# Turning a block's keys with VectorE and memory in a gated attention block: unscaled keys, scales applied on the way out of PSUM

## The chip, the cores and the metric

The kernel runs on one core of one Trainium2 chip. The metric is the device time of one execution in microseconds (us). Before the change the median of three runs was 1321.52 us (1321.27 to 1323.14).

## The reference, cut to what matters

All data are float32. There are 32 batches of 256 query tokens and 77 context tokens, 256 wide. A batch first passes a cross attention with 8 heads of 128 features, without softmax, and then a feed-forward part with 16 small heads and a softmax. The change touches the cross attention alone:

```python
f_q, f_k, f_v = proj(q), proj(k), proj(v)       # layer norm, @ w_in.T, 8 heads of 128; k and v are the same context
cosine_sim = dots / (qn[..., :, None] * kn[..., None, :])
q_ratio = 2.0 * minimum(q_var, 1.0) / (q_var + 1.0)      # k_ratio likewise
var_component = einsum('hqn,hqm->hqnm', q_ratio, k_ratio)
mixed = cw * cosine_sim + vw * cosine_sim * decorr_scale + ww * var_component
out = einsum('hqnm,hqmd->hqnd', mixed, f_v)               # then @ w_out.T + b_out
```

The weights `cw`, `vw`, `ww` and `decorr_scale` are one number for each head. So a score of head h, query n and key m is (dot of the query, divided by its norm, with the key) x (a scale of h and m) + (q_ratio of h and n) x (k_ratio of h and m, times `ww`). As keys and values are equal, the scale can be put on the keys, half (a square root) in the scores and half in the values, or wholly on the scores.

## The kernel before, in words

A preamble (to about 70 us of the profile) loads and turns the weights, normalizes the context and gathers the means that the head weights need. The batches then run in a software pipeline. The list `cycle`, written out by hand, gives the order of the stages of one round: an entry `(2, scale_keys)` in round n calls `scale_keys` for batch n + 2. `run` calls each stage once for each batch, so stages that the preamble has called are passed over. The last two rounds have lists of their own (`last_but_one`, `last`). Instructions of TensorE (`pe`), ScalarE (`act`), VectorE (`dve`) and GpSimd (`pool`) stay on their engine in the order of the program; the DMAs on SyncE's queue (`nc.sync`) are placed by the tile framework, and the profile shows some of them ahead of their place in the list.

Matmul results go to PSUM tiles: three tiles `mm` of 128 x 512, two tiles `sc` for the softmax scores, one `zp`. A float32 matmul is two MATMUL instructions in the trace, a transpose on TensorE is one.

For the context of batch b the stages are these. `key_features` multiplies a part of the normalized context by `w_in` (ScalarE copies it to `fvx`). `count_keys` and `measure_keys` take each token's variance and norm for each head. `align_keys` copies the 77 rows of the batch to `fv`, and their norms and ratios (16 numbers a row) to `nr`. `weigh_keys` multiplies these by the head weights `aw`. `scale_keys` (VectorE) lays the scales out as diagonal blocks `dk`. `transpose_keys` multiplies `fv` by `dk` on TensorE, eight matmuls of 96 columns (16 instructions), which turns and scales the keys in one step and adds the ratios as a column; ScalarE and VectorE copy one half each to `fvT`. `key_outputs` multiplies `fvT` by `w_out` into `vw`, in three stages: two in which each matmul fills 64 PSUM partitions with the first 64 (`MA`) keys of a head, and one (pair 2) with 32 partitions for the last 13 (`MR`) keys of all heads.

For the queries, `query_features` makes `fq`, `scale_queries` takes ratios and norms and divides by the norms (GpSimd), and `turn_queries` turns `fq`: from batch 2 on VectorE transposes blocks of 32 x 32, one DMA writes them to memory (`fd`) and `fetch_queries` reads them back in another order to `fqT`. The ratios ride along as a ninth head. `query_scores` has the same three stages as `key_outputs`; ScalarE and VectorE copy the results to `s`. `attend` multiplies `s` by `vw`, adds the residual, and the feed-forward part follows: `ff_stats`, `ff_norm`, `ff_transpose`, `ff_project`, `ff_values`, then four turns of `scores` (TensorE, then VectorE's maximum `nm`), `exponents` (ScalarE), `scale_values` (VectorE) and `mix_values` (TensorE), then `ff_out`, `ff_gelu` and `ff_add`.

Of the kernel before, what the change touches and what calls it, by code (L numbers as in the profile page):

```python
# [35 lines left out]
def gated_block_kernel(  # L36
# [59 lines left out]
    nquart = const.tile([P, H], F32, name="nquart")  # L96
    dve.memset(nquart, -0.25)
# [207 lines left out]
    def measure_keys(b):  # L305

        run(b, count_keys)
        for i in range(halves_due(b - 1) // 2, halves_due(b) // 2):
            rows = min(P, NCTX - i * P)
            nr = nrx[0:rows, i % 4, :]  # L310
            m2, n2, rt = head_stats(key_stats.pop(i), "k")
            pool.tensor_tensor(nr[:, 0:H], n2, nquart[0:rows], ALU.pow)
            dve.scalar_tensor_tensor(nr[:, H : 2 * H], m2, P - 1.0, rt, ALU.min, ALU.mult)

    def align_keys(b):
        k = kept[b]
        k["fv"] = sw.tile([P, 4, D], F32, tag="ct", name="fv", bufs=2).rearrange(
            "p a d -> p (a d)"
        )[0:M]
        k["nr"] = pa.tile([M, 2 * H], F32, tag="nr", name="nr")  # L320
        at = 0
        while at < M:
            i, row = divmod(b * M + at, P)
            n = min(P - row, M - at)
            nc.sync.dma_start(out=k["fv"][at : at + n], in_=fvx[i % 4][row : row + n])
            nc.sync.dma_start(out=k["nr"][at : at + n], in_=nrx[row : row + n, i % 4, :])
            at += n

# [6 lines left out]
    SL = MA + 32  # L335

    def weigh_keys(b):

        k = kept[b]
        k["dk"] = pa.tile([M, H // 2, 2, SL], F32, tag="dk", name="dk", bufs=1)  # L340
        pool.tensor_tensor(k["nr"], k["nr"], aw[0:M].rearrange("p w h -> p (w h)"), ALU.mult)

    def scale_keys(b):

        k = kept[b]
        dve.tensor_tensor(
            k["dk"],
            eyes.unsqueeze(1).to_broadcast([M, H // 2, 2, SL]),
            k["nr"][:, 0:H].rearrange("m (g i) -> m g i", i=2).unsqueeze(3).to_broadcast(
                [M, H // 2, 2, SL]  # L350
            ),
            ALU.mult,
        )
        for i in range(2):
            dve.tensor_copy(
                k["dk"][:, :, i, M + 16 * i], k["nr"][:, H + i : 2 * H : 2]
            )

    def transpose_keys(b, hh):
        k = kept[b]  # L360
        if hh == 0:
            k["fvT"] = pa.tile([P, H, SL], F32, tag="fvT", name="fvT", bufs=2)
        pt = mm_tile()
        for i in range(4):
            h = hh * 4 + i
            pe.matmul(
                pt[:, i * SL : (i + 1) * SL], lhsT=k["fv"][:, h * P : (h + 1) * P],
                rhs=k["dk"][:, h // 2, h % 2, :], start=True, stop=True,
            )
        out = k["fvT"][:, hh * 4 : hh * 4 + 4, :].rearrange("p h m -> p (h m)")  # L370
        (act.copy if hh == 0 else dve.tensor_copy)(out, pt[:, 0 : 4 * SL])

    def paired(pt, k, pair, rhs):

        for c in range(2):
            for i in range(2):
                h = 4 * pair + 2 * c + i
                pe.matmul(
                    pt[MA * i : MA * (i + 1), c * S : (c + 1) * S],
                    lhsT=k["fvT"][:, h, 0:MA], rhs=rhs(h), start=True, stop=True,  # L380
                )

    def key_outputs(b, pair):

# [5 lines left out]
        if pair < 2:  # L390
            paired(pg, k, pair, lambda h: woutT[:, h, :])
            out = k["vw"][:, 2 * pair : 2 * pair + 2, :].rearrange("p g c -> p (g c)")
            (act.copy if pair == 0 else dve.tensor_copy)(out, pg)
            return
        for i in (1, 0):
            for j in range(4):
                n = 32 if i else MR + 1
                pe.matmul(
                    pg[32 * j : 32 * j + n, 0:D], lhsT=k["fvT"][:, 2 * j + i, MA : MA + n],
# [4 lines left out]
    def query_scores(b, pair):  # L404

# [4 lines left out]
        if pair < 2:  # L410
            paired(pg, k, pair, lambda h: k["fqT"][:, :, h, :])
            out = k["s"][:, 2 * pair : 2 * pair + 2, :].rearrange("p g q -> p (g q)")
            (act.copy if pair == 0 else dve.tensor_copy)(out, pg)
            return
        for i in (1, 0):
            for j in range(4):
                n = 32 if i else MR
                pe.matmul(
                    pg[32 * j : 32 * j + n, 0:S], lhsT=k["fvT"][:, 2 * j + i, MA : MA + n],
                    rhs=k["fqT"][:, :, 2 * j + i, :], start=(i == 1), stop=(i == 0),  # L420
                )

        dve.scalar_tensor_tensor(
            k["s"][:, 4, :].rearrange("p (i a) -> p i a", a=32),
            pg[:, 0:S].rearrange("p (i a) -> p i a", a=32), scored[:, 0:1],
            k["fqT"][:, :, H, :], ALU.mult, ALU.add,
        )
# [21 lines left out]
    def scale_queries(b, t):  # L449
# [12 lines left out]
            qrps[t][:, :, MR], m2, P - 1.0, rt, ALU.min, ALU.mult  # L462
        )

    def turn_queries(b, t):
# [3 lines left out]
        if t == 0:  # L469
            k["fqT"] = pa.tile([P, S // 32, H + 1, 32], F32, tag="fqT", name="fqT", bufs=1)  # L470
        ratios = qrps[t].rearrange("p h w -> p (h w)")
        if b < 2:
# [11 lines left out]
            pt = mm_tile()  # L484
            pe.transpose(pt[:, 0:P], ratios, ident)
            dve.tensor_copy(
# [1091 lines left out]
```

## Time and profile before

| what | value |
|---|---|
| median of three runs | 1321.52 us |
| the profiled execution: its time, its span | 1320.74 us, 1318.7 us |
| busy PE / DVE / ACT / POOL | 1294.0 / 1042.7 / 880.6 / 508.7 us |
| granted TensorE clock | 0.999 |
| one round, from `mix_values` (u 3) to the next | 36.73 us in most rounds; 38.45 us with two halves of `key_features` |
| DMA queue q1 | 144.42 MB, 35.8% of 16 engines |

The profile names an instruction by engine, operation and tiles, `out<-in`, with its shape; `zp<-e,vz 128*32 128x256` is a matmul with 32 columns of weights and 256 moving columns. All instructions that go through the ordering helper carry its line, 32, so groups are told apart by tile. SPq is SyncE's queue of DMAs and shows the line of the DMA itself. The timeline merges neighbours of a kind: start, duration of the merged piece, and the count behind the x.

### The profile page before, as it was taken

To read this page: it belongs to the slowest core of one execution; us is meant where nothing else is said; L and a number is where in the kernel's file an instruction comes from. 1 tells how busy PE (TensorE), PEld (TensorE's weight loads), DVE (VectorE), ACT (ScalarE), POOL (GpSimd) and SP (SyncE) were. 2 spreads that over 40 slices of the span, in tenths; PEclk is the share of its full clock that TensorE was granted. 3 is DMA by queue.
4 is the path that set the end of the run, shared out by engine and by line. 5 is a ranking of instruction groups with operands and counts; after the bars stand their busy time and mean duration, and the time that the engine had idled before them with its cause. 6 is when DMAs were issued, how large, how long until landed. Compare 5 with 4: busy or idle time off the path is not lost.

```text
span 1318.7 us, 26220 instructions
## 1 busy us (share of the span) xinstructions
PE 1294.0 (98%) x8671; PEld 777.1 (59%) x8671; DVE 1042.7 (79%) x3071; ACT 880.6 (67%) x2856; POOL 508.7 (39%) x629
## 2 busy tenths in 40 slices
PE   8999999999999999999999999999999999999998
PEld 7865556665555556665555556665555555655554
DVE  7746788788788787888887887878887877888865
ACT  6822557677666767667666767676666767667666
POOL 6823443434334342435333443433433433343300
PEclk9999999999999999999999999999999999999999
DMA  8610034432244343433343443432343433432231
GB/s 279 212 35 22 20 113 122 127 115 98 83 129 127 118 126 115 125 116 100 95 120 120 129 123 119 126 115 94 95 127 120 126 116 102 133 98 85 69 97 41
DMA packets 99638, 146.11 MB, mean 111 GB/s; under 512 B 14170, under 2 KB 65039, under 8 KB 99502
## 3 DMA queue, kind: packets, MB, share of 16 engines
q1 hardware_dynamic: 98670, 144.42, 35.8%
q8 instruction: 69, 1.13, 0.4%
q14 instruction: 67, 0.55, 0.1%
q10 hardware_dynamic: 832, 0.00, 0.0%
HBM read 65.98 MB, written 68.16 MB: 102 GB/s over the span
## 4 chain that ended last, share of the span: by engine, by line
PE 91%; DVE 4%; DMA 3%; POOL 1%; ACT 1%; issue 1%; SPq 0%; ACTq 0%; DVEq 0%; POOLq 0%
PE mm L32 70%; PE sc L32 11%; PE zp L32 9%; DVE nm L32 1%; DMA x<-in_x_dram 1%; DVE st L32 1%; DMA w_in_n<-in_L_xattn_w_in_dram 1%; DVE qst L32 0%; DMA ct<-in_ctx_dram 0%; ACT e L32 0%; DVE qt L32 0%; DMA out_dram<-x 0%; POOL rstd_x L32 0%; DMA gcol<-in_L_xattn_ln_g_dram 0%; POOL rc L32 0%
## 5 line engine op out<-in xcount | busy, mean ns | idle before, releaser
L32 ACT ACTIVATE e<-sc,nm 128x256 f32<-128x256 f32 x1016 | 468.3, 483 | 221.2 <-DVE nm L32 221.1
L32 DVE TENSOR_REDUCE nm<-sc 128x4 f32<-128x1024 f32 x254 | 299.2, 1219 | 48.2 <-PE sc L32 48.1
L32 PE MATMUL mm<-winT,xTc 128*128 128x512 f32 x512 | 234.6, 599 | 0.3 <-ACT fqT L32 0.3
L32 ACT ACTIVATION_READ_ACCUMULATOR e<-sc,nm 128x1 f32 x1016 | 217.6, 214 | 0.0
L32 POOL TENSOR_TENSOR rq<-qt,nhalf 128x8 f32<-128x8 f32 x64 | 105.4, 1647 | 256.8 <-DVE qt L32 256.8
L32 PEld LDWEIGHTS mm<-winT,xTc 128*128 128x128 f32 x512 | 94.2, 190 | 105.3 <-issue 95.7
L32 PE MATMUL sc<-q,kTf 32*128 32x512 f32 x1016 | 147.6, 640 | 0.5 <-ACT kTf L32 0.5
L32 PE MATMUL mm<-vw,s 128*128 128x256 f32 x640 | 146.7, 384 | 0.0
L32 PE MATMUL zp<-e,vz 128*32 128x256 f32 x2048 | 137.0, 385 | 0.3
L32 PEld LDWEIGHTS mm<-vw,s 128*128 128x128 f32 x640 | 119.0, 190 | 28.4 <-issue 13.5
L32 POOL TENSOR_TENSOR fq<-fq,rq 128x1024 f32<-128x1024 f32 x64 | 121.4, 1897 | 5.0
L32 PEld LDWEIGHTS zp<-e,vz 128*32 128x32 f32 x2048 | 53.4, 109 | 105.0 <-issue 34.5
L32 POOL TENSOR_TENSOR nrx<-kt,nquart 128x8 f32<-128x8 f32 (+1 forms) x20 | 32.9, 1644 | 194.8 <-DVE kt L32 194.8
L32 DVE BATCH_NORM_STATS2 qst<-fq 128x6 f32<-128x128 f32 x512 | 104.7, 280 | 0.0
L32 PE MATMUL mm<-fqT,fvT 128*64 128x256 f32 (+2 forms) x1024 | 94.3, 385 | 3.5 <-DMA nr<-nrx 1.9
L32 PE MATMUL mm<-woutT,fvT 128*64 128x256 f32 (+2 forms) x1024 | 93.7, 382 | 1.5 <-ACT v L32 1.5
L32 DVE RECIPROCAL sums<-sums 128x8 f32<-128x8 f32 x128 | 23.7, 185 | 75.1 <-ACT e L32 75.1
L32 PEld LDWEIGHTS mm<-fqT,fvT 128*64 128x64 f32 (+2 forms) x1024 | 46.7, 119 | 58.6 <-DVE qst L32 22.0
L32 ACT ACT_TABLE_LOAD x60 | 77.0, 1283 | 4.9 <-DMA x<-in_x_dram 4.2
L32 POOL TENSOR_SCALAR xn<-x,mv_x,rstd_x 128x256 f32<-128x256 f32 x64 | 78.5, 1233 | 4.2 <-issue 4.2
L32 ACT COPY fvx<-mm 128x512 f32<-128x512 f32 (+1 forms) x40 | 23.5, 587 | 80.4 <-PE mm L32 80.4
L32 PE MATMUL mm<-winT,kT_all 128*128 128x512 f32 (+1 forms) x160 | 74.8, 598 | 0.0
(239 smaller groups left out, 2135.4 us busy)
## 6 DMA issues: line engine op xcount, KB each, us to landing
fd<-fb SPq DMA_DIRECT2D x60, 576.0 KB
fqT<-fd SPq DMA_DIRECT2D x240, 144.0 KB
x<-in_x_dram SPq DMA_DIRECT2D x64, 256.0 KB
x_kept<-x SPq DMA_DIRECT2D x32, 256.0 KB
z_kept<-zT SPq DMA_DIRECT2D x32, 256.0 KB
out_dram<-x SPq DMA_DIRECT2D x31, 256.0 KB
xd<-xb SPq DMA_DIRECT2D x29, 256.0 KB
xq<-xd SPq DMA_DIRECT2D x116, 64.0 KB
```

Of the source, the lines that this page charges most:

```text
L32: return lambda *args, **kw: self._tc.keep_in_program_order(method(*args, **kw))
```

## The change

Keys are no longer scaled before they are turned. `measure_keys` takes the full power -1/2 instead of -1/4. `align_keys` splits the last 13 keys over two sets of rows (even and odd heads), `turn_keys` turns the rows as `turn_queries` does (VectorE, memory, `fetch_keys`; TensorE in the first two batches). The scales and ratios travel through memory (`align_norms`, `fetch_norms`) into one number for each row of the score tiles, and the queries' ratios are spread through memory over those rows (`spread_ratios`, `sort_ratios`, `fetch_ratios`); GpSimd multiplies them (`weigh_ratios`). All five score tiles leave PSUM by a VectorE instruction that multiplies by the scale and adds that product. All products with `fvT` have 32 columns. Before the rounds, a square root on GpSimd (`hw`) is gone and four small VectorE instructions make `aw_rows`. In `cycle`, `turn_keys` stands near the start, `ff_gelu` and its table load before `scores` 2, and `scores` 3 before `ff_transpose`.

```diff
 def measure_keys(b):
-            pool.tensor_tensor(nr[:, 0:H], n2, nquart[0:rows], ALU.pow)
+            pool.tensor_tensor(nr[:, 0 : 2 * H : 2], n2, nhalf[0:rows, 0:H], ALU.pow)
...
+            if at < MA:
+                n = min(n, MA - at)
+                nc.sync.dma_start(out=k["fv"][at : at + n], in_=fvx[i % 4][row : row + n])
+            else:
+                for odd in range(2):
+                    to = at + 16 * odd
+                    nc.sync.dma_start(
+                        out=k["fv"][to : to + n].rearrange("m (g i d) -> m g i d", i=2, d=P)[
+                            :, :, odd
+                        ],
...
+    def align_norms(b):
...
+            nc.sync.dma_start(out=nr[at : at + n], in_=nrx[row : row + n, i % 4, :])
...
+        k["nd"] = nd = dram.tile([P, 5, 2], F32, tag="nd", name="nd")
+        for i in range(2):
+            nc.sync.dma_start(
+                out=nd[MA * i : MA * (i + 1), 0:4, :],
+                in_=nr[0:MA].rearrange("m (g i w) -> i m g w", i=2, w=2)[i],
+            )
+        nc.sync.dma_start(
+            out=nd[:, 4, :].rearrange("(h m) w -> m h w", m=16),
+            in_=nr[MA : MA + 16].rearrange("m (h w) -> m h w", w=2),
+        )
+    def fetch_norms(b):
...
+        nc.sync.dma_start(out=k["rows"], in_=k.pop("nd"))
 def weigh_keys(b):
+        k["wr"] = pa.tile([P, 5, 2], F32, tag="wr", name="wr")
+        pool.tensor_tensor(k["wr"], k["rows"], aw_rows, ALU.mult)
-    def scale_keys(b):
...
-    def transpose_keys(b, hh):
...
-                pt[:, i * SL : (i + 1) * SL], lhsT=k["fv"][:, h * P : (h + 1) * P],
-                rhs=k["dk"][:, h // 2, h % 2, :], start=True, stop=True,
...
+    def turn_keys(b):
+        k["fvT"] = pa.tile([P, 3, H, 32], F32, tag="fvT", name="fvT", bufs=2)
+        if b < 2:
...
+                    pe.transpose(
+                        pt[:, i * SL : (i + 1) * SL], k["fv"][:, h * P : (h + 1) * P],
+                        ident[0:SL, 0:SL],
+                    )
...
+        kb = pa.tile([P, 4, H, 32], F32, tag="fb", name="kb", bufs=2)[0:SL]
+        dve.transpose(
+            kb.rearrange("p j h a -> p h j a"),
+            k["fv"].rearrange("p (h j a) -> p h j a", j=4, a=32),
+        )
+        kd = dram.tile([SL, 4, H * 32], F32, tag="kd", name="kd")
+        nc.sync.dma_start(out=kd, in_=kb.rearrange("p j h a -> p j (h a)"))
+    def fetch_keys(b):
...
+        for j in range(4):
+            nc.sync.dma_start(
+                out=k["fvT"][32 * j : 32 * j + 32].rearrange("p i h a -> p i (h a)"),
+                in_=kd[:, j].rearrange("(i p) n -> p i n", p=32),
+            )
 def paired(pt, k, pair, rhs):
         for c in range(2):
-            for i in range(2):
-                h = 4 * pair + 2 * c + i
+            for j in range(4):
+                h = 4 * pair + 2 * c + j // 2
                 pe.matmul(
-                    pt[MA * i : MA * (i + 1), c * S : (c + 1) * S],
-                    lhsT=k["fvT"][:, h, 0:MA], rhs=rhs(h), start=True, stop=True,
+                    pt[32 * j : 32 * j + 32, c * S : (c + 1) * S],
+                    lhsT=k["fvT"][:, j % 2, h, :], rhs=rhs(h), start=True, stop=True,
 def key_outputs(b, pair):
-            (act.copy if pair == 0 else dve.tensor_copy)(out, pg)
+            act.copy(k["vw"][:, 2 * pair : 2 * pair + 2, :].rearrange("p g c -> p (g c)"), pg)
 def query_scores(b, pair):
-            (act.copy if pair == 0 else dve.tensor_copy)(out, pg)
...
+        for g in (2 * pair, 2 * pair + 1) if pair < 2 else (4,):
+            c = g % 2
+            dve.scalar_tensor_tensor(
+                k["s"][:, g, :], pg[:, c * S : (c + 1) * S], k["wr"][:, g, 0:1],
+                k["rq"][:, g, :], ALU.mult, ALU.add,
+            )
+    def spread_ratios(b):
+        rb = pa.tile([P, 32], F32, tag="rb", name="rb")
+        dve.transpose(rb, qrs[b % 2])
+        k["rc"] = dram.tile([P, 32], F32, tag="rc", name="rc")
+        nc.sync.dma_start(out=k["rc"], in_=rb)
+    def sort_ratios(b):
+        k["rd"] = dram.tile([H * NT, 4, 32], F32, tag="rd", name="rd")
+        nc.sync.dma_start(
+            out=k["rd"], in_=k.pop("rc").rearrange("(i c) a -> c i a", c=32)[0 : H * NT]
+        )
+    def fetch_ratios(b, first):
+        if first:
...
+            k["re"] = dram.tile([P, S], F32, tag="re", name="re")
...
+            k["rq"] = pa.tile([P, 5, S], F32, tag="rqr", name="rqr", bufs=1)
+            for i in range(2):
...
+                nc.sync.dma_start(
+                    out=k["rq"][MA * i : MA * (i + 1), 0:4, :],
+                    in_=src.unsqueeze(0).to_broadcast([MA, 4, S]),
+                )
+        else:
+            nc.sync.dma_start(out=k["rq"][:, 4, :], in_=k.pop("re"))
+    def weigh_ratios(b):
+        for g in range(5):
+            r = k["rq"][:, g, :]
+            if g < 4:
+                pool.tensor_scalar(r, r, k["wr"][:, g, 1:2], None, ALU.mult)
+            else:
+                pool.tensor_scalar(
+                    r, r, k["wr"][:, g, 1:2], ident[:, MR + 1 : MR + 2], ALU.mult, ALU.add
+                )
 def turn_queries(b, t):
-        dve.transpose(fb[:, :, H, :], ratios.rearrange("p (j a) -> p j a", a=32))
-        fd = dram.tile([P, 4, (H + 1) * 32], F32, tag="fd", name="fd")
+        fd = dram.tile([P, 4, H * 32], F32, tag="fd", name="fd")
...
-    run(0, scale_keys)
     run(0, scale_queries, 1)
-    run(0, transpose_keys, 0)
-    run(0, transpose_keys, 1)
+    run(0, spread_ratios)
+    run(0, sort_ratios)
+    run(0, fetch_ratios, True)
+    run(0, fetch_ratios, False)
+    run(0, weigh_ratios)
+    run(0, turn_keys)
...
     cycle = [
         (4, load_queries),
+        (1, fetch_ratios, False),
         (-1, mix_values, 3),
         (0, scores, 0),
         (2, measure_keys),
-        (2, align_keys),
         (3, norm_inputs),
         (0, exponents, 0, 0),
+        (2, align_keys),
         (-1, ff_out),
         (-1, ff_keep),
+        (2, turn_keys),
         (0, exponents, 0, 1),
...
+        (2, align_norms),
         (-1, ff_norm_inv),
+        (1, weigh_ratios),
         (0, scores, 1),
...
+        (2, fetch_keys),
...
         (3, transpose_inputs),
+        (2, fetch_norms),
+        (-1, ff_gelu),
+        (2, warm_exponentials),
+        (0, square_weights),
         (0, scale_values, 1),
-        (2, weigh_keys),
         (1, query_scores, 0),
...
-        (2, scale_keys),
         (1, attend, 0),
...
-        (2, transpose_keys, 0),
-        (2, transpose_keys, 1),
         (1, ff_norm, 1),
         (2, scale_queries, 1),
+        (2, spread_ratios),
         (3, key_features),
+        (0, scores, 3),
         (1, ff_transpose),
-        (-1, ff_gelu),
-        (2, warm_exponentials),
-        (0, scores, 3),
         (0, mix_values, 2),
-        (2, key_outputs, 2),
         (2, key_outputs, 0),
         (2, key_outputs, 1),
+        (2, key_outputs, 2),
         (2, turn_queries, 0),
+        (2, sort_ratios),
...
         (1, ff_project, "q"),
+        (2, weigh_keys),
...
         (2, fetch_queries, 0),
+        (2, fetch_ratios, True),
         (2, fetch_queries, 1),
...
```

## The prediction, made before the result was known

> **What bounds the kernel now.** I read the page first: the busy shares and the chain that ended last.
>
> ```profile
> PE 1294.0 (98%) x8671; PEld 777.1 (59%) x8671; DVE 1042.7 (79%) x3071; ACT 880.6 (67%) x2856; POOL 508.7 (39%) x629
> PE 91%; DVE 4%; DMA 3%; POOL 1%; ACT 1%; issue 1%; SPq 0%; ACTq 0%; DVEq 0%; POOLq 0%
> ```
>
> TensorE is busy for 98% of the span and carries 91% of the chain. Then the timeline of one round, which begins at the `zp` group (`mix_values`, u 3) at 551.23 and ends at the next one at 587.96:
>
> ```profile
> 551.23 1.07 PE L32 MATMUL zp<-e,vz 128*32 128x256 f32 x16
> 552.23 1.14 PE L32 MATMUL sc<-q,kTf 32*128 32x512 f32 x8
> ...
> 564.36 2.95 PE L32 MATMUL mm<-fqT,fvT 128*64 128x256 f32 x32
> 567.24 1.14 PE L32 MATMUL sc<-q,kTf 32*128 32x512 f32 x8
> 568.31 1.07 PE L32 MATMUL zp<-e,vz 128*32 128x256 f32 x16
> 569.31 4.58 PE L32 MATMUL mm<-vw,s 128*128 128x256 f32 x20
> 573.73 1.92 PE L32 MATMUL mm<-dk,fv 77*128 77x96 f32 x16
> 575.49 1.91 PE L32 MATMUL mm<-winT,kT_all 128*128 128x512 f32 x4
> 577.24 0.60 PE L32 MATMUL mm<-ident,xf 128*128 128x128 f32 x4
> 577.77 1.14 PE L32 MATMUL sc<-q,kTf 32*128 32x512 f32 x8
> 578.84 1.07 PE L32 MATMUL zp<-e,vz 128*32 128x256 f32 x16
> 579.73 2.92 PE L32 MATMUL mm<-woutT,fvT 128*32 128x256 f32 x32
> ```
>
> No piece waits: each starts where the one before ends. So a round is the sum of TensorE's work, 36.73 us, and what the change takes from TensorE comes off, until another engine is late. How near the others are, the table by stretches shows (us; PE, PEld, DVE, ACT and POOL busy, with counts):
>
> ```profile
> 551.23:587.96 36.73, 36.73 (x254) 21.55 (x253) 31.54 (x97) 25.75 (x86) 14.99 (x16) 1.00 0.39 118
> ```
>
> VectorE has 5.2 us to spare in such a round (in rounds that have no keys to count it works less: 28.8 in 245.38 to 282.11).
>
> **TensorE, step by step.** (1) The keys' product with `dk` goes: from 573.73 to 575.49, 1.76 us, in 30 batches: -52.8. (2) In batches 0 and 1 eight transposes take its place: 32 transposes of `fq` are busy 4.2 us, 0.13 each, so 1.05 instead of 1.76, twice, and a little less for 96 columns: -1.6. (3) Four transposes of ratios go, 1.3 busy: -1.3. (4) The 64-column products become twice as many of 32. By the groups' busy time that costs: 64 columns, 62.3/512 = 0.122 us each, eight to a stage, 0.97; 32 columns (`zp`), 137.0/2048 = 0.067, sixteen to a stage, 1.07; four such stages in 32 batches, +12.8. But by the starts of single matmuls in the trace, two of 64 columns start together every 0.209 to 0.216 us, and four of 32 columns every 0.216: both stages take four such beats. What differs is the passage between widths: the last beat before a change lasts 0.309, and the second start after a change to 64 columns comes after 0.260 instead of 0.209. Each of `query_scores` and `key_outputs` now loses its inner passage, 0.093 + 0.044 = 0.137 us, twice in 32 batches: -8.8. I take this end, since a busy mean charges the passages around a lone `zp` stage to its sixteen instructions; the other end stays for the range. (5) `ff_transpose` now stands between `scores` 3 and `mix_values`, so there are two passages more (0.093 before, 0.104 on the first full-width instruction: 0.320 instead of 0.216), 0.2 in 30 rounds: +6.0. Sum: -58.5; a round falls from 36.73 to 34.90.
>
> **VectorE.** Off, for a batch: `dk` 0.94 and its two copies 0.24, the copies of `fvT` 0.56, `vw` 0.69, `s` 0.69, the old last step of `s` 0.48, two ratio transposes 0.54: 4.1. On: the transpose of 96 x 1024, priced as that of `fq` (1.22); five steps of 128 x 256 out of PSUM at 0.476 (the row of the old last step), 2.4; a transpose of 128 x 32, between the smallest rows (0.16) and 128 x 128 (0.27), I take 0.2: 3.8. So 31.5 becomes 31.2 of 34.9 and the spare time falls to 3.7 us. It hides only if it lies at the right places; I walked the new order with these durations, TensorE's stages set end to end from 0:
>
> - `query_scores` occupies TensorE from 13.1 to 15.9. VectorE is done with `scale_queries`, the turn of `xn` and `scale_values` at 16.3, needs five steps 0.41 apart (starts of neighbours), done at 18.4. `attend` starts at 17.9 and needs the fifth tile at 18.8: hidden, by 0.4.
> - The maximum of `scores` 2 then starts at 18.4, later in the round than before (568.41 - 551.23 = 17.2, the start of that row in VectorE's timeline), while TensorE reaches `ff_transpose` earlier: its second half wants `xf` at 25.45 and has it at 25.4. Nothing to spare.
> - `scale_queries` (t 1) and the maximum of `scores` 3 end at 30.7; ScalarE, rid of table loads there (1.28 each), ends `exponents` at 33.9, `scale_values` is done at 34.5, `mix_values` wants it at 34.9.
> - `count_keys` and `ff_add` end at 36.9, the next round's first maximum can start at 34.9 + 2.2 = 37.1.
>
> All fits, twice by less than 0.3. If my placing is off by half a microsecond it costs that much; I charge 0.2 for each of 30 rounds: +6.
>
> **ScalarE** loses 0.59 + 0.48 and gains 0.59 (25.3 of 34.9). **GpSimd** gains five products of 128 x 256, between 0.555 (`xTc`, two operations with column scalars) and 1.233 (`xn`, the same shape): 2.8 to 6.2 us a round; I take 0.56, as `xTc` multiplies too. It has 20 us free. Behind `weigh_ratios` in its queue stand `rq` and `fq` of `scale_queries` t 0 (wanted by `turn_queries` only at 31), ahead of it the `i` step, which waits for ScalarE until about 8.
>
> **DMAs.** A round has some 22 issues on SP's queue, 0.3 to 0.8 us each; 16 or so come on top (one `kd`, four of `fetch_keys`, two or three more of `fv`, three `nd`, one `rows`, `rc`, `rd`, `re`, three `rq`), 17 us of 35 in all; in bytes about +1.4 MB (`kd` twice 0.39, `rq` 0.64) on 4.1 MB, with DMA engines 39% busy. A hop through memory is seen here:
>
> ```profile
> 567.10 0.33 SPq L246 DMA_DIRECT2D xd<-xb  x1
> 569.11 1.74 SPq L248 DMA_DIRECT2D xq<-xd  x4
> ```
>
> 2.0 us from issue to the next issue that needs it (2.8 for `fd`, the largest). The longest new chain is the ratios': `rb` at 28.6, four hops of 2.0 to 2.8 (`rc`, `rd`, `re`, `rq`) to 36.6 to 39.8, GpSimd to 39.4 to 46.0, wanted by `query_scores` at 34.9 + 16.3 = 51.2: hidden by 5 us or more, if SP issues each when it is ready. The keys' chain (`fv`, `kd`, `fvT`) ends near 14 and is wanted at 26.9. The cover is gone at two places only. Before the rounds, batch 0 has the same chain open: its ratios are there at about 109.4 (110.3 before, less `dk`), the last product at 119.5, and `attend` would start 1.6 us earlier than now (120.06): about +2 (0 to +6 with slower hops and products). In the round before the last, `query_scores` starts after 7.4 us and already waits 1.6 for its DMA: +1, as the queue is longer (0 to +3).
>
> **A rule against the change.** VectorE takes all five `s` tiles in 5 x 0.41 = 2.1 us while TensorE makes them in 2.7. The Trainium skill (TensorEngine Tiling (Array Packing), section Performance Considerations) says that once tiling has sped TensorE up, emptying PSUM may become the limit, and that both ScalarE and VectorE should be used for it; here ScalarE's share is taken away. By the row VectorE keeps pace; by the rule the 1.2 us by which the maximum of `scores` 2 now starts later (18.4 instead of 17.2) would reach TensorE, 36 us in 30 rounds, and the sum would be 1308. Also, DMA: Bandwidth & Descriptors (Specifications) wants pieces of 512 B or more in memory; `nd` writes 8 B pieces. No row here shows such a write.
>
> **The sum.** 1320.7 (the profiled execution) - 58.5 + 6 + 2 + 1 = 1271.2; that execution is 0.8 below the median of the runs: 1272.
>
> **Rivals.**
>
> *VectorE sets the round.* For: 31.2 of 34.9, its order is fixed, and two places have no spare time. Against: the rounds without keys to count have 2.7 us less for it. If the heavy rounds take 36 and the passage gain of (4) fails (12.8 instead of -8.8), that is 15 to 22 us more: 1284 to 1310.
>
> *Data that come through memory too late* (slower than before). VectorE stands still in its queue at `turn_keys` until `fv` has landed, or at `query_scores` until the ratios are weighed; behind it wait the maxima, so ScalarE and TensorE. SP's queue is in order too: 17 us of issues and six more hops of about 2 us, if each blocked what stands behind it, would fill 29 of 35 us, and the ratios would come some 5 to 9 us later. It decides from 1.9 us a round (58.5 over 30 rounds); I price it at 2.5 to 4: 1271 + 75 to 120 = 1346 to 1391, nearest 1346. Against: the profile shows `fv` issued at 578.05, ahead of its place in the list, so the queue's order follows what is ready.
>
> *The products don't shrink:* a wait before `key_outputs` (for `fvT`) takes the place of the 1.76 us. `fvT` has 12 us to spare, so this is only 1321 with a small chance.
>
> **Chances.** Forecast (1256 to 1284) 0.55; VectorE sets the round (1284 to 1312) 0.26; about no change 0.02; slower 0.17. The range 1256 to 1312 leaves out the slower end. A change within 0.2%, what a measurement of this kernel can tell, gets 0.02; faster 0.81, slower 0.17.
>
> **What would show it.** Right: rounds of about 34.9 us, no `mm<-dk,fv`, `fqT,fvT` and `woutT,fvT` all 128*32 with four starts together, `zp` without waits. Wrong: PE busy under 96%; TensorE's weight loads (PEld) waiting for VectorE's `xf`, `s` or `vz`; VectorE waiting for a DMA (`fv`) or GpSimd (`rq`); the 32-column stages longer than 0.9 us each. The forecast falls if a round takes over 35.6.

## The result, and the profile after

The changed kernel takes 1333.37 us (median of four runs, 1331.82 to 1337.76), beside 1321.41 us for the kernel before (four runs, 1321.27 to 1323.14): a ratio of 1.0093, with a 95% interval of 1.0067 to 1.0118. It is slower by 0.9%. The forecast was 1272 us, faster. The profiled execution after took 1331.82 us with a span of 1330.0.

The page of the changed kernel: the busy shares, the DMA queue of SyncE (packets, MB, share of the 16 DMA engines), the chain that ended last, and the row of `query_scores` (count, busy us, mean ns, idle us just before and what ended it):

```profile
PE 1253.8 (94%) x9195; PEld 731.1 (55%) x9195; DVE 1038.6 (78%) x3009; ACT 871.3 (66%) x2826; POOL 643.9 (48%) x785
q1 hardware_dynamic: 179454, 186.47, 53.5%
PE 68%; DMA 15%; DVE 6%; SPq 4%; issue 2%; POOL 2%; ACT 1%; ACTq 0%; DVEq 0%; POOLq 0%
L32 PE MATMUL mm<-fqT,fvT 128*32 128x256 f32 (+1 forms) x1536 | 103.8, 425 | 44.1 <-DMA rqr<-re 17.6
```

TensorE works 40 us less than before (1294.0), and its share of the chain falls from 91% to 68%. What came in is DMA (15%, before 3%) and SyncE's queue (4%, before 0%). So the work was saved, and the saving was spent on waiting for memory.

The timeline of TensorE shows both halves. An undisturbed round, from `zp` at 625.60 to `zp` at 660.38:

```profile
625.60 1.07 PE L32 MATMUL zp<-e,vz 128*32 128x256 f32 x16
...
635.10 3.70 PE L32 MATMUL mm<-winT,xTc 128*128 128x512 f32 x8
638.73 2.80 PE L32 MATMUL mm<-fqT,fvT 128*32 128x256 f32 x48
...
660.38 0.85 PE L32 MATMUL zp<-e,vz 128*32 128x256 f32 x12
```

34.78 us, nothing waits; before it was 36.73. And a disturbed round, which takes 41.60 us (1.7 of them a second half of `key_features`):

```profile
884.19 1.07 PE L32 MATMUL zp<-e,vz 128*32 128x256 f32 x16
...
893.70 3.70 PE L32 MATMUL mm<-winT,xTc 128*128 128x512 f32 x8
900.73 4.48 PE L32 MATMUL mm<-fqT,fvT 128*32 128x256 f32 x48 [3.33 <-DMA rqr<-re]
```

`query_scores` should start 13.13 us into the round, at 897.32; it starts at 900.73, and its 48 matmuls then take 4.48 us instead of 2.80. The idle 3.33 and these 1.7 make the 5 us that the round loses. (The releaser named, `rqr<-re`, is a DMA issued just behind the last `fqT`. In the trace its landing ends at 901.15, when TensorE already works; that of the last `fqT`, which TensorE reads, ends at 900.64.) The slow matmuls are a matter of the clock, as the table by stretches says (us; PE, PEld, DVE, ACT, POOL busy with counts; granted clock; DMA share; GB/s):

```profile
625.37:660.15 34.78, 34.78 (x270) 19.65 (x268) 28.76 (x77) 25.45 (x86) 15.72 (x19) 1.00 0.61 168
883.96:900.50 16.54, 13.44 (x74) 5.85 (x72) 12.45 (x32) 12.76 (x44) 3.33 (x5) 1.00 0.80 206
900.97:904.38 3.41, 3.41 (x37) 2.15 (x33) 0.95 (x3) 1.19 (x2) 3.33 (x4) 0.50 0.75 246
904.38:908.00 3.62, 3.62 (x44) 1.70 (x37) 2.97 (x5) 0.36 (x1) 1.57 (x1) 1.00 0.56 160
```

After the idle 3.33 us the granted clock is 0.50 for 3.41 us, then 1.00 again; half of 3.41 us is the 1.7 us that the 48 matmuls take longer.

Why `fqT` was late stands in the timeline of SyncE's queue. First the good round (start 625.60): each DMA with its issue time.

```profile
617.52 0.34 SPq L375 DMA_DIRECT2D rows<-nd  x1
...
619.38 0.32 SPq L480 DMA_DIRECT2D rc<-rb  x1
622.85 0.56 SPq L485 DMA_DIRECT2D rd<-rc  x1
624.79 0.69 SPq L494 DMA_DIRECT2D re<-rd  x1
625.59 1.16 SPq L583 DMA_DIRECT2D fd<-fb  x2
...
629.21 1.75 SPq L592 DMA_DIRECT2D fqT<-fd  x4
...
631.66 2.33 SPq L592 DMA_DIRECT2D fqT<-fd  x4
...
634.51 0.43 SPq L508 DMA_DIRECT2D rqr<-re  x1
```

Then the disturbed one (start 884.19), and below it the two steps of VectorE that make `rb` and `fb`:

```profile
875.96 0.60 SPq L367 DMA_DIRECT2D nd<-nr  x1
...
881.81 0.34 SPq L375 DMA_DIRECT2D rows<-nd  x1
882.25 0.38 SPq L800 DMA_DIRECT2D x_kept<-x  x1
882.72 0.37 SPq L480 DMA_DIRECT2D rc<-rb  x1
883.14 0.79 SPq L359 DMA_DIRECT2D nr<-nrx  x1
884.51 0.61 SPq L485 DMA_DIRECT2D rd<-rc  x1
886.49 0.69 SPq L494 DMA_DIRECT2D re<-rd  x1
887.28 0.88 SPq L583 DMA_DIRECT2D fd<-fb  x2
...
890.73 1.94 SPq L592 DMA_DIRECT2D fqT<-fd  x4
...
893.40 2.29 SPq L592 DMA_DIRECT2D fqT<-fd  x4
```

```profile
877.05 0.21 DVE L32 STREAM_TRANSPOSE rb<-qr 128x32 f32<-128x32 f32 x1
879.75 2.36 DVE L32 STREAM_TRANSPOSE fb<-fq 128x1024 f32<-128x1024 f32 x2
```

`rows` stands at the head of the queue until `nd` has landed, so `rc` goes out 5.5 us after `rb` is done. `rd` then waits for `rc`, `re` for `rd`, and only then `fd` is issued: 5.2 us after both `fb` were done (882.11). It was ready, and it stood in line. In the good round the same line costs `fd` 1.4 us. The waits of SyncE's queue over the whole run add this up (total us, times, longest; the line is that of the waiting DMA, L485 of `rd`, L375 of `rows`, L494 of `re`):

```profile
SPq L485 <- DMA rc<-rb: 43.0, 20, 5.2
SPq L375 <- DMA nd<-nr: 36.2, 22, 3.8
SPq L494 <- DMA rd<-rc: 33.8, 28, 2.5
```

By place, the 11.4 us of span that were lost: the first round starts at 182.84 instead of 179.97 (+2.9); the 29 rounds that follow take 1076.2 instead of 1076.4 (-0.2, though 29 x 1.94 = 56 were saved); the round before the last takes 37.57 instead of 30.79 (+6.8); the last one is equal, and the end after it is 1.9 longer.

In the 29 rounds the loss can be counted in full. The rows are of these rounds in the changed kernel and in e2b, a kernel of the next section whose rounds are all even:

```profile
182.84:1259.04 1076.20, 1030.98 (x7790) 582.21 (x7789) 880.52 (x2497) 742.11 (x2445) 535.27 (x594) 0.99 0.58 150
174.42:1192.03 1017.61, 1016.37 (x7789) 572.06 (x7788) 874.19 (x2497) 741.89 (x2445) 538.08 (x598) 1.00 0.47 135
```

Of the 58.6 us between them TensorE is idle for 44.0 and busy for 14.6. Of its idle time in the changed kernel 38.2 us lie in 14 waits at `query_scores`; and it works for 24.9 us at half clock, which makes 12.5 us of the longer busy time. The issue of the second `fd` tells which rounds wait: the 14 in which it goes out 1.4 us after the round's start or later all do, the 15 in which it goes out by 0.9 us don't.

### The profile page after: what moved, and what is told of

It is laid out like the page before. It is cut to its first block, busy times and chain, and to the rows that moved or that the text cites. A ratio compares the mean times of both kernels' runs of the same rounds, so it can differ in the third digit from the quotient of the medians.

```text
span 1330.0 us, 28175 instructions
## 1 busy us (share of the span) xinstructions
PE 1253.8 (94%) x9195; PEld 731.1 (55%) x9195; DVE 1038.6 (78%) x3009; ACT 871.3 (66%) x2826; POOL 643.9 (48%) x785
## 4 chain that ended last, share of the span: by engine, by line
PE 68%; DMA 15%; DVE 6%; SPq 4%; issue 2%; POOL 2%; ACT 1%; ACTq 0%; DVEq 0%; POOLq 0%
PE mm L32 52%; PE sc L32 9%; PE zp L32 7%; DMA fqT<-fd 2%; DMA fd<-fb 2%; DMA rqr<-re 2%; DMA rc<-rb 2%; DMA z_kept<-zT 1%; DVE nm L32 1%; SPq L592 1%; DVE qt L32 1%; DMA xq<-xd 1%; ACT e L32 1%; DMA rd<-rc 1%; DVE qst L32 1%
## 5 line engine op out<-in xcount | busy, mean ns | idle before, releaser
L32 ACT ACTIVATION_READ_ACCUMULATOR e<-sc,nm 128x1 f32 x1016 | 221.8, 218 | 0.0
L32 POOL TENSOR_SCALAR rqr<-rqr,wr 128x256 f32<-128x256 f32 x128 | 117.1, 934 | 79.7 <-DMA rqr<-rd 68.9
L32 PE MATMUL mm<-vw,s 128*128 128x256 f32 x640 | 149.6, 390 | 4.5 <-DVE s L32 4.5
L32 PE MATMUL mm<-fqT,fvT 128*32 128x256 f32 (+1 forms) x1536 | 103.8, 425 | 44.1 <-DMA rqr<-re 17.6
L32 PEld LDWEIGHTS mm<-fqT,fvT 128*32 128x32 f32 (+1 forms) x1536 | 55.1, 118 | 100.0 <-DVE vz L32 17.5
L32 POOL TENSOR_TENSOR nrx<-kt,nhalf 128x8 f32<-128x8 f32 (+1 forms) x20 | 32.9, 1647 | 153.7 <-DVE kt L32 153.7
L32 DVE SCALAR_TENSOR_TENSOR s<-mm,wr,rqr 128x256 f32<-128x256 f32 x160 | 67.9, 477 | 36.9 <-PE mm L32 22.7
L32 POOL TENSOR_SCALAR rs<-mv 128x1 f32<-128x1 f32 x64 | 14.8, 231 | 158.8 <-DVE mv L32 117.7
L32 PE MATMUL mm<-woutT,fvT 128*32 128x256 f32 (+1 forms) x1536 | 89.3, 379 | 1.7 <-DMA fvT<-kd 0.7
L32 PEld LDWEIGHTS sc<-q,kTf 32*128 32x128 f32 x1016 | 41.3, 185 | 75.8 <-issue 33.2
```

Of the source, the lines that this page charges most:

```text
L32: return lambda *args, **kw: self._tc.keep_in_program_order(method(*args, **kw))
```

## The experiments

The table gives for each kernel the median, the ratio to the kernel before with its interval, and from the trace the start of the first round, the 29 rounds after it and the round before the last (us). A kernel whose rounds are nearly all even and free of waits has 1017 to 1020 in the fifth column.

| kernel | median | ratio | first round | 29 rounds | next |
|---|---|---|---|---|---|
| before | 1321.4 | 1 | 180.0 | 1076.4 | 30.8 |
| after | 1333.4 | 1.0093 [1.0067, 1.0118] | 182.8 | 1076.2 | 37.6 |
| e4: before, 32 columns | 1312.6 | 0.9932 [0.9915, 0.9949] | 179.9 | 1069.1 | 30.6 |
| e3: no `nd`, `rows` | 1281.2 | 0.9695 [0.9676, 0.9714] | 180.7 | 1028.5 | 36.1 |
| e2b: no ratios by memory | 1259.1 | 0.9532 [0.9513, 0.9551] | 174.4 | 1017.6 | 31.1 |
| e6: fewer bytes for `rq` | 1277.9 | 0.9673 [0.9654, 0.9693] | 178.8 | 1027.3 | 35.9 |
| e9: `nd` as plain rows | 1288.3 | 0.9742 [0.9725, 0.9759] | 182.8 | 1036.1 | 36.7 |
| e7: keys by TensorE | 1335.6 | 1.011 [1.009, 1.013] | 182.6 | 1082.3 | 37.1 |
| e1: `fd`, `fqT` first | 1306.7 | 0.9889 [0.9873, 0.9906] | 181.0 | 1054.6 | 35.0 |
| e10: e1, `rows` late | 1314.6 | 0.9938 [0.992, 0.9957] | 181.7 | 1062.7 | 37.6 |
| e11: e10, `nd` late | 1285.4 | 0.9733 [0.9716, 0.975] | 181.4 | 1032.5 | 35.3 |
| e5: `fd` first, `rows` late, `fv` early | 1269.3 | 0.9611 [0.9595, 0.9627] | 180.1 | 1018.7 | 35.3 |
| e8: e5, shorter path of ratios | 1269.1 | 0.9602 [0.9578, 0.9626] | 179.2 | 1019.8 | 34.9 |

### Is the sum of TensorE right? (e4, e2b)

e4 is the kernel before with step (4) alone:

```diff
-            for i in range(2):
-                h = 4 * pair + 2 * c + i
+            for j in range(4):
+                h = 4 * pair + 2 * c + j // 2
...
-                    pt[MA * i : MA * (i + 1), c * S : (c + 1) * S],
-                    lhsT=k["fvT"][:, h, 0:MA], rhs=rhs(h), start=True, stop=True,
+                    pt[32 * j : 32 * j + 32, c * S : (c + 1) * S],
+                    lhsT=k["fvT"][:, h, 32 * (j % 2) : 32 * (j % 2) + 32], rhs=rhs(h),
+                    start=True, stop=True,
```

> The kernel before with one part of the change alone: the first two stages of key_outputs and query_scores as 32-column products (twice as many). By the starts of single matmuls (four of 32 columns together in one beat of 0.216 us, one passage of widths fewer, 0.137 us, in each of 64 stage groups): 8.8 us less, about 1312.7 us. By the mean busy time of a group (0.067 against 0.122 us): 12.8 us more, about 1334 us.

Its rounds take 36.427 us in place of 36.728: 0.301 less a round, and 8.8 us less over the run. The end that the prediction took (-8.8) is the right one; the other end (+12.8) is out.

e2b keeps the instructions of TensorE, VectorE, ScalarE and GpSimd, but the ratios don't go through memory: `rc`, `rd`, `re` and `rq` are gone, and GpSimd multiplies a constant tile.

```diff
 def fetch_ratios(b, first):
         if first:
+            kept[b]["rq"] = pa.tile([P, 5, S], F32, tag="rqr", name="rqr", bufs=1)
...
 def weigh_ratios(b):
-            r = k["rq"][:, g, :]
+            r, c = k["rq"][:, g, :], winT[:, 0, 0:S]
```

> The changed kernel without the DMAs of the queries' ratios (rc, rd, re, rq); GpSimd's five products read a weight tile in their place, so the result differs. Queue order as the framework places it. Theory (queue order): fd goes out when VectorE is done; no stall at query_scores, and the stall of batch 0 is gone: 1262 to 1275 us. Rival (rows and nd alone): with the ratios gone rows still stands ahead of fd in the queue, 1275 to 1295 us.

All 29 rounds are even, the first starts 8.4 us earlier than in the changed kernel, and the round before the last takes 31.1. What the changed kernel loses hangs on those six DMAs, or on what they do to others in the queue. (Without them the framework also issues `rows` elsewhere: in about half the batches 16 to 17 us into a round, where the changed kernel has it 2 to 16 us before one starts.) VectorE has as much to do as in the changed kernel and no round waits for it.

### What holds up the queue? (e3, e6, e9)

e3 leaves out the norms' way through memory (`nd`, `rows`); GpSimd weighs a constant instead.

```diff
-        k["nd"] = nd = dram.tile([P, 5, 2], F32, tag="nd", name="nd")
...
 def fetch_norms(b):
-        nc.sync.dma_start(out=k["rows"], in_=k.pop("nd"))
+        if not rowc:
+            rowc.append(const.tile([P, 5, 2], F32, name="rowc"))
+            pool.memset(rowc[0], 0.5)
+        kept[b]["rows"] = rowc[0]
```

> The changed kernel without the trip of the keys' scales through memory (nd, 640 pieces of 8 bytes, and rows): a constant stands for them, so the result differs; the ratios' chain stays as it is. Theory A (the waits of rd and re stand ahead of fd): part of the loss stays, as rd still waits for rc and re for rd, 1290 to 1315 us. Theory B (rows, which waits about 5 us for nd to land, holds back rc, and only that makes the chain late): 1268 to 1285 us. If neither, 1325 to 1335 us.

The 29 rounds fall by 47.7 us, to within 11 of the even ones, by leaving out four small DMAs (10 KB written and read for a batch). The time is in theory B's range; but three waits at `query_scores` remain, 8.1 us in all, so `rows` was not the only thing ahead of `fd`.

e6 keeps every hop and the order, but reads 128 KB instead of 512 KB of `rq` for a batch (one of four row groups; the other three products take a constant).

```diff
-                    out=k["rq"][MA * i : MA * (i + 1), 0:4, :],
-                    in_=src.unsqueeze(0).to_broadcast([MA, 4, S]),
+                    out=k["rq"][MA * i : MA * (i + 1), 0, :],
+                    in_=src[0].unsqueeze(0).to_broadcast([MA, S]),
```

> The changed kernel, with the same hops and the same order, but the two large rq reads fetch one group of four (128 KB in place of 512 KB a batch; GpSimd reads a weight tile for the other three, so the result differs). Theory (queue order): bytes don't matter, 1320 to 1335 us. Rival (DMA engines too full): the stalls shrink by about the share of bytes, 1300 us or less.

This takes away 48.9 us of the 29 rounds, so the theory that bytes don't matter is out. But the line in the queue is as long as before: the second `fd` goes out 0.5 us after the round's start (median; 0.3 in the changed kernel), more than 2 us after it in 11 rounds (13), and `rd` waits 42.7 us for `rc` (43.0). What is shorter is the way of `fqT` itself: in the rounds that still wait for it, `query_scores` starts 3.3 to 4.3 us after the issue of the last `fqT`, where the changed kernel has 4.7 to 6.1. With the second `fd` 1.9 to 2.4 us after the round's start none of e6's four rounds waits, and each of the changed kernel's three does. So by these rows the stall has two halves: `fd` is issued late, and the reads behind it take long while the bytes of `rq` are under way.

e9 writes `nd` as 96 plain rows of 64 B by one DMA and has the 8 B pieces on the read side, three DMAs. Bytes, hops and the number of issues are the same.

```diff
-        for i in range(2):
-            nc.sync.dma_start(
-                out=nd[MA * i : MA * (i + 1), 0:4, :],
-                in_=nr[0:MA].rearrange("m (g i w) -> i m g w", i=2, w=2)[i],
-            )
...
+        nc.sync.dma_start(out=nd, in_=nr)
 def fetch_norms(b):
+        for i in range(2):
+            nc.sync.dma_start(
+                out=rows[MA * i : MA * (i + 1), 0:4, :],
+                in_=nd[0:MA].rearrange("m (g i w) -> i m g w", i=2, w=2)[i],
+            )
...
```

> The changed kernel with its own order, but nd is written as 96 plain rows of 64 B by one DMA, and the 8 B pieces are on the read side (three DMAs from nd to rows instead of three writes and one read). The number of issues is the same. Theory A (8 B writes land late, up to 9 us after their issue, and rows waits for them at the head of SyncE's queue): the wait of rows for nd falls from a median of 4.6 us to about 2.5, fd is issued 2 us earlier in the disturbed rounds, and the 56 us of stalls shrink to 20 to 40: 1295 to 1315. Theory B (the landing is late because of all that is queued, not because of the piece size): the wait stays, or moves to the reads, and the time stays at 1325 to 1340.

The 29 rounds fall by 40.1 us; the time is below theory A's range, so this way of moving `nd` saves more than it had. The median wait from the last `nd` to `rows` falls from 4.6 to 3.7 us, less than expected, but the late cases go: `rd` is issued by 3.2 us before the round's start in three rounds of four, where the changed kernel issues it at the start or later in one of four. The Trainium skill (DMA: Bandwidth & Descriptors, Specifications) says that a write of less than 512 B makes the DMA engine read and modify as well; e9 speaks for that direction. No run here splits its part from that of having one write to wait for in place of three.

### Is it the order? (e1, e10, e11, e5)

All four pin DMAs of SyncE's queue in the order in which the list has them, by a dependence without a semaphore on the DMA pinned before. e1 pins `rc`, `fd`, `rd`, `fqT`, `re` and `rq`, and moves the ratios behind the queries:

```diff
+    def in_turn(ins):
+        if pinned:
+            tc.add_manual_dep(ins.ins, pinned[-1].ins.name, ...)
+        pinned.append(ins)
...
-        (2, sort_ratios),
         (2, turn_queries, 1),
+        (2, sort_ratios),
         (2, fetch_queries, 0),
-        (2, fetch_ratios, True),
         (2, fetch_queries, 1),
+        (2, fetch_ratios, True),
```

> The changed kernel, with the same DMAs and bytes, but the order of issue on SP's queue is fixed for one group: the queries' writes (fd, both) and reads (fqT, all eight) go ahead of the ratios' second and later hops (rd, re, rq). Theory (queue order): in the changed kernel fd stands ready at about -2.5 us before the round and is issued up to 8 us later, behind the waits of rd for rc and of re for rd; so fqT lands too late. Then the stalls at query_scores go, nearly all rounds take 34.8 us, and the time is 1270 to 1285 us. Rival (transfers too many: 186 MB, DMA engines 54% busy): the same bytes move, fqT lands as late, 1325 to 1335 us. Rival (VectorE's place for turn_keys): unchanged, 1325 to 1335 us.

`query_scores` hardly waits in the rounds any more (1.0 us in all), but the time is 1306.7, above the theory's 1270 to 1285: the stall went to the next transfer in line. VectorE's waits show it:

```profile
DVE kb L32 <- DMA fv<-fvx: 23.2, 4, 7.1
```

In four rounds `turn_keys` waits up to 7.1 us for `fv`, now issued behind the last `rq`; this is the place that the slower rival had named. It is made by this order; the changed kernel has no such wait. There `turn_keys` waits five times, 12.0 us in all, for `fd` to be read out of `fb`, since `kb` takes one of the two buffers that `fb` has: a late `fd` holds up VectorE too.

e10 adds that `rows` is fetched behind the last `rq`, half a round later, and weighed then:

```diff
         (1, fetch_ratios, False),
+        (1, fetch_norms),
...
-        (2, fetch_norms),
...
+        (1, weigh_keys),
         (1, weigh_ratios),
...
-        (2, weigh_keys),
```

> The first reordering (fd and fqT ahead of rd, re, rq) with one more change: rows is fetched half a round later, behind the last rq. fv stays where the list has it. It tells apart which of the two further moves of the 1269 us version did the work. If the wait of rows for nd at the head of the queue was what made fv late in the first reordering (1306.7), the rounds become even here too, and the time is 1270 to 1280. If fv was late because it is issued behind rd, re and rq, VectorE's kb still waits for fv in some rounds (7 us each there), and the time is 1290 to 1307.

It missed both expectations: 1314.6, slower than e1, and the waits for `fv` are down to one of 2.1 us. VectorE now waits for `rqr` at `s`, 75 times. SyncE's queue in its round that starts at 582.5:

```profile
578.19 1.29 SPq L374 DMA_DIRECT2D nd<-nr  x2
...
580.83 1.44 SPq L594 DMA_DIRECT2D fd<-fb  x2
582.32 1.40 SPq L496 DMA_DIRECT2D rd<-rc  x1
587.70 3.64 SPq L603 DMA_DIRECT2D fqT<-fd  x8
```

With `rows` gone from the head, `nd` and parts of `fv` are issued right ahead of `fd`, and `fqT` waits long for `fd`: 4.2 us (median of the third to the twenty-eighth round) from the second `fd` to the first `fqT`, where the kernel before has 1.5. From the first `fd`, whose data that read needs, it is 4.8 against 2.8, as the two `fd` go out closer together here. e11 pins the three `nd` writes behind `rows` as well:

```diff
-            nc.sync.dma_start(
+            in_turn(nc.sync.dma_start(
                 out=nd[MA * i : MA * (i + 1), 0:4, :],
...
```

> The version that fetches rows late (1314.6 us), with one more pin: the three writes of nd stay behind rows in SyncE's queue, where the list has them. In that version they had moved forward, to 3.3 us before to 2.8 us after the round's start, just ahead of fd, and from the issue of the second fd to the first fqT it took 4.2 us (median), where the kernel before and the 1269 us version have 1.5 to 1.6 and issue the nd writes elsewhere. fv stays where the framework puts it. Theory (the 8 B writes hold up whatever is issued right behind them, so fd): that hop falls to 1.5 to 2 us, rq is fetched some 3 us earlier, the s steps no longer wait for GpSimd, and the time is 1268 to 1280. Rival (the fv reads in front of fd, up to 300 KB, are what fd waits for): the hop stays near 4 us and the time stays at 1300 to 1315.

Between theory and rival: that hop falls to 2.6 us (3.2 from the first `fd`), the time by 29 us to 1285.4. The next kernel differs from e11 in the place of `fv`, with `spread_ratios` one stage later to let it pass (its `nd` is not pinned, but is mostly issued at the same place, some 10 to 18 us into the round), and takes 16 us less.

e5 is e10 with `fv` pinned too, a round earlier, ahead of `rc`:

```diff
-        (2, align_keys),
...
-        (2, spread_ratios),
         (3, key_features),
+        (3, align_keys),
+        (2, spread_ratios),
```

> The changed kernel, same DMAs and bytes, with three places on SP's queue fixed: fd, fqT ahead of rd, re, rq (as in e1_order); fv for a batch issued a round earlier, ahead of rc (in e1_order fv came after the ratios and VectorE's kb waited for it); rows a round later, behind the last rq, so that nothing stands behind its wait for nd. Theory (the loss is the order of waits on one queue, and each fix alone moves it to the next hop): stalls in the rounds go, 34.8 us each; 1330 less 56 in the rounds and about 3 in the last, 1268 to 1278 us. Rival (the DMA engines are too full): at least a third of the loss stays, 1290 us or more.

1269.3 us, with every DMA and byte of the changed kernel. Its page, and its queue in the same stretch of a round (start 567.2):

```profile
PE 1238.0 (98%) x9195; PEld 719.3 (57%) x9195; DVE 1038.4 (82%) x3009; ACT 869.7 (69%) x2826; POOL 643.7 (51%) x785
q1 hardware_dynamic: 179454, 186.47, 52.1%
```

```profile
564.63 1.45 SPq L594 DMA_DIRECT2D fd<-fb  x2
566.17 0.60 SPq L496 DMA_DIRECT2D rd<-rc  x1
567.31 3.67 SPq L603 DMA_DIRECT2D fqT<-fd  x8
...
574.97 0.48 SPq L386 DMA_DIRECT2D rows<-nd  x1
...
577.26 1.29 SPq L374 DMA_DIRECT2D nd<-nr  x2
```

`fd` is issued when `fb` is there, its hop takes 1.6 us again (median), and `rows` and `nd` come when nothing waits behind them. It is 4.8% faster than the changed kernel (1269.25 / 1333.37) and 3.9% faster than the kernel before.

### Fewer DMAs, shorter paths (e7, e8)

e7 lets TensorE transpose the keys in all batches, so that `kd` and four `fvT` reads go.

```diff
-        if b < 2:
+        if b < B:
```

> The changed kernel with the keys turned by TensorE in all batches (eight transposes, 0.83 us a round, and two copies out of PSUM in place of VectorE's kb, the DMA kd and four DMAs fvT): five DMAs and 768 KB fewer a round. Theory (the ratios' and norms' hops hold up fd): the stalls at query_scores stay, 1325 to 1355 us (25 us of transposes more, some relief of the queue). Rival (the keys' own trip through memory is the cause): 1285 to 1300 us.

The time rises to 1335.6, but for a cause of its own: only two waits at `query_scores` remain (2.0 and 0.9 us), while most rounds take 36.9 us, as the eight transposes (0.82 us) come on top and the matmuls behind them wait 1.2 us for ScalarE to empty their PSUM tile. The waits for `fqT` shrink, but a round that is 2.1 us longer gives the queue more time as well, and no run here parts the two; on the price of the memory route it says nothing.

e8 is e5 with `rd` written from `rb` by four DMAs, without the hop through `rc`, and with the four one-operation products on GpSimd as multiply-and-add:

```diff
-        in_turn(nc.sync.dma_start(out=k["rc"], in_=rb))
+        for i in range(4):
+            in_turn(nc.sync.dma_start(out=k["rd"][:, i, :], in_=rb[32 * i : 32 * i + H * NT, :]))
...
-                pool.tensor_scalar(r, r, k["wr"][:, g, 1:2], None, ALU.mult)
+                pool.tensor_scalar(r, r, k["wr"][:, g, 1:2], zero, ALU.mult, ALU.add)
```

> The version with the new order of SyncE's queue, with two steps of the ratios' path made shorter: four DMAs write the 16 wanted rows of rb straight into rd, so the hop rc to rd goes; and the four one-operation products on GpSimd (0.93 us each in the changed kernel) become multiply-and-add with a column of zeros, the form of the fifth product (0.56). Theory (what is left of the loss is the length of the ratios' path where nothing covers it): the rounds stay at 34.79; before the first round and in the round before the last, the path is 2 us (a hop) and 1.5 us (4 x 0.37) shorter less 1 us for three more issues, so 1269.3 falls by 2 to 5, to 1264 to 1267, and the four products take 0.56 each. Rival (the path before the first round is not what sets it; the 0.93 us belong to the shape): the products stay at 0.93 and the time stays at 1269 or so.

The four products in the changed kernel's page, and those of e8 in the answer for the tile (minimum/median/maximum ns):

```profile
L32 POOL TENSOR_SCALAR rqr<-rqr,wr 128x256 f32<-128x256 f32 x128 | 117.1, 934 | 79.7 <-DMA rqr<-rd 68.9
```

```profile
L32 POOL TENSOR_SCALAR rqr<-rqr,wr,zero x128: 547/554/595, 119.9 to 1212.6; 128x256 f32<-128x256 f32 x128
```

The form with two operations takes 0.55 us, that with one 0.93: the theory's half on GpSimd holds. The time doesn't follow (1269.1, 1265.8 to 1272.1). In the profiles 0.9 us are gained before the first round and 0.3 in the round before the last, and the rounds give 1.1 back.

## Why the prediction was wrong

**TensorE's sum held.** An undisturbed round takes 34.79 us; 34.90 was forecast. Over the 29 rounds its busy time falls from 1072.9 us in the kernel before to 1016.4 in e2b, by 56.5. Step (4) is confirmed by itself in e4.

**VectorE's cover held.** In the heavy rounds of e5 that take 34.8 us it is busy 31.1 to 31.5 us (30.6 in the first; forecast 31.2), and e2b's even rounds show that the two places without spare time did not bind. The charge of 6 us was not needed, and the rival *VectorE sets the round* is out. So is the sum of 1308: VectorE alone empties all five tiles in time. The Trainium skill's rule to use both engines for it (TensorEngine Tiling (Array Packing), Performance Considerations) did not bind here.

**The step that failed is the paragraph on DMAs**, in the words "hidden by 5 us or more, if SP issues each when it is ready". Two things were wrong in it. SyncE does not issue what is ready; it stands at the DMA that comes next until that one's data are there. The argument against the slower rival (one `fv` seen ahead of its place in the list, "so the queue's order follows what is ready") took an order that the framework had laid down for one that is found at run time. The waits of the kernel before would have told it (total us, times, longest):

```profile
SPq L498 <- DVE fb L32: 230.9, 60, 9.4
```

SyncE stood waiting for each of the 60 `fb` there, with nothing urgent behind them. And the working followed the new chain alone. It asked when the ratios arrive, and not who stands behind their waits: `fd` and `fqT`, which had been issued on time in nearly every round before. The chain was also taken as too short: four hops of 2.0 to 2.8 us make 8.0 to 11.2, but even in the good round above the last read of `rq` is issued 15.1 us after `rc`, with the eight `fqT` reads ahead of it.

**The slower rival had the right mechanism and a wrong place and price.** Data came through memory too late, but at TensorE's `query_scores` for `fqT`, and, but for single waits, neither at `turn_keys` nor for the ratios. Its price was 2.5 to 4 us a round; 2.0 were lost (1076.2 - 1017.6 = 58.6 over 29), just above its point of 1.9, 44.0 of the 58.6 as waits and 12.5 by the half clock after long ones. So the rounds broke even.

**Terms that were too small**: GpSimd's product, taken at 0.56 and measured at 0.93 (0.55 for the fifth), inside the bounds; it lies on the ratios' path at the two open ends. Before the rounds about nothing was forecast in all (+2 for the ratios' path, less what TensorE saves there), and the first round starts 2.9 us later; in e2b it starts 8.4 earlier than in the changed kernel, so the open path costs more than the bound of 6. The round before the last is 6.8 longer, for +1 (0 to +3); e2b gives back 6.5 of them. Both are the ratios' path, and e5 takes off 2.7 and 2.3 by order alone.

**Left open:** why a disturbed round follows one that is not, with the same list; and the 1.9 us by which the end came later after the last round (1.7 to 2.3 in e1, e2b, e5 and e10 as well, none in e4), though the last store is issued 5.8 us after that round in both.

## What to carry to other kernels

A DMA queue is an engine with its own order: for each transfer that a change puts into it, ask what it waits for and which older transfer stands behind that wait, and give each of those its slack; then lay the queue's order down by hand as one does for the engines, with waiting hops of a chain spread between transfers that are ready. A chain of hops should be costed with the bytes and small pieces that will be under way beside it, and not from the shortest hop of a quiet queue. A new tile that takes a buffer of an old one, as `kb` does of `fb`, ties the two chains together. Here the same DMAs and bytes cost 1333 or 1269 us, by the order in which they are issued.

## What the runs showed of the hardware

- What is issued just ahead of a hop changes its length: from the first `fd` to the first `fqT` 2.8 us in the kernel before, 3.2 in e11, 4.8 in e10, where writes of `nd` in pieces of 8 B and parts of `fv` go out right ahead (medians of the third to the twenty-eighth round; 2.8, 3.2 and 4.3 over all 30 batches).
- After 3.33 us without work TensorE's granted clock was 0.50 over 3.41 us. In the 29 rounds of the changed kernel all seven waits of 3.08 to 3.93 us came with such a stretch (one of twice the length), and the two of 2.56 and 3.05 us did not. The Trainium skill (TensorE: Matmul & The Clock Gate, What's actually happening) tells of half the clock, for about 3.4 us, after an idle window of about 3.4 us; the length agrees, while here an idle time of 3.08 us was enough.
- A GpSimd TENSOR_SCALAR of 128 x 256 takes 0.93 us with a multiplication alone (`rqr`), 0.55 with a multiplication and an addition, and 1.24 with a subtraction and a multiplication (`xn`): the number of operations doesn't tell the time.
